# The causal mask of the attention maxima: by TensorE products with an identity, or inside VectorE's maximum instruction

## The chip, the cores and the metric

One Trainium2 chip, one of its cores. The metric is the device time of one launch in microseconds; lower is better. Times before the change are the median of three runs.

## The reference, cut to what matters

A two-layer post-norm decoder over 16 sequences of 512 tokens with 256 features. Each layer has causal self-attention, cross attention to 64 context tokens and a feed-forward part (a mixture of experts in layer 0, a wide hidden layer with sines in layer 1). The change concerns the causal self-attention of both layers, 16 heads of 16 features each:

```python
q, k, v = (heads(q), heads(k), heads(v))               # (batch, 16 heads, 512 tokens, 16)
logits = jnp.einsum('bhqd,bhkd->bhqk', q, k) * scale   # layer 0 adds a position bias
causal = jnp.tril(jnp.ones((t, t), dtype=bool))
logits = jnp.where(causal[None, None], logits, -jnp.inf)
attn = jax.nn.softmax(logits, axis=-1)
out = jnp.einsum('bhqk,bhkd->bhqd', attn, v)
```

## The kernel before, in words

**Recording and planning.** The kernel does not emit instructions as it goes. Each stage of each sequence records operations with an engine, a cost in microseconds and what they read and write. `stage` gives each operation a rank from the place of its stage and from a pair of offsets per kind of stage (`at`, `to`). `run_plan` then places all operations of all stages in one list, engine by engine, taking the earliest possible start and among those the lowest rank, and holding to the number of buffers of each pool. It emits them in that order, and every engine works through its own queue in that order. So the work of several sequences and stages is interleaved: between two pieces of one attention TensorE does expert products, projections or feed-forward products of others. All pinned instructions are issued by one helper line, which is why the profile names L347 for nearly everything; groups are told apart by their tiles.

**Causal attention** (`causal_attention`). The 16 heads are four groups of four heads; a group's heads lie on 32 partitions each. The scores are computed twice. The first time they are laid out with queries on partitions (`pa<-k,q` in the profile), only to find each query's maximum: `max_unit` fills one PSUM tile `pa` of 2 × 512 columns, one half for each head of a pair, and VectorE takes the maxima into `m`. The second time they are laid out with keys on partitions (`pa<-q,k`), in `exp_unit`: the maxima are subtracted (layer 0 through products `pa<-mrow,minus`, layer 1 inside `q` and `k`), ScalarE takes the exponential into `e`, GpSimd sets the part above the diagonal to zero, and TensorE multiplies by the values (`po<-e,vp`).

**Units.** A query block is 128 queries; block i needs the keys of blocks 0 to i, `kw = (i + 1) * 128` columns. `wide_banks` packs blocks into units of 512 columns per head: kind 0 is block 3 alone (512), kind 1 is blocks 2 and 0 (384 + 128), kind 2 is block 1 of two groups (256 + 256). With 16 sequences, two layers, and two pairs of groups and ten units per pair of groups (five kinds and groups, two pairs of heads) there are 640 max units and 640 exp units, each of 2 × 512 columns.

**Masking before.** In a max unit the last 128 columns of each block are the diagonal, where keys later than the query must not count. After the score products `masks()` adds a matrix of 0 and −1e30 there, by bf16 products with an identity that accumulate onto the scores in PSUM: one product per head and diagonal (kind 1's 384 block ends next to the 128 block's only columns, so that one product of 256 columns covers both diagonals). Then one `tensor_reduce` per block takes the maxima of both heads.

**Steps.** One step of the attention is one TensorE operation of one max unit and one exp unit (`score`), or of two of one kind when the other kind is not at hand. Its products run in three parts: the score products of all its units, then the maxima's subtraction, then the masks. Two `pa` tiles exist, so the next step's score products wait until VectorE has reduced the max unit and ScalarE has read the exp unit. When a group's maxima are complete, GpSimd copies them into a wide tile (`parts` in layer 0, `whole` in layer 1), TensorE transposes that (`pr`), and the group's exp units can begin.

Of the kernel before, what the change touches and what calls it, by code (L numbers as in the profile page):

```python
# [33 lines left out]
P = 128  # L34
# [36 lines left out]
def decoder_kernel(ctx: ExitStack, tc: tile.TileContext, a: dict, out: bass.AP):  # L71
# [15 lines left out]
    def whole_rows(key, name, shape):  # L87
# [17 lines left out]
    ident = const.tile([P, P], F32, tag="ident", name="ident")  # L105
    make_identity(nc, ident)

    cmask16 = const.tile([P, 2, P], BF16, tag="cmask16", name="cmask16")
    nc.gpsimd.memset(cmask16, 0.0)
    nc.gpsimd.affine_select(  # L110
        out=cmask16, in_=cmask16, compare_op=ALU.is_ge,
        fill=MASKED, base=0, pattern=[[0, 2], [-1, P]], channel_multiplier=1,
    )
    cmask16 = cmask16.rearrange("p n k -> p (n k)")

    vp = const.tile([P, NT, H, 2 * HD], F32, tag="vp", name="vp")
    nc.gpsimd.memset(vp, 1.0)
# [190 lines left out]
    def stage(place, record, *args):  # L308


        stage_ops.clear()
        record(*args)

        for t in loads.get(record.__name__, ()):
            for n in writers.get(t, ()) if isinstance(t, str) else ():
                for o in stage_ops:
                    if o.engine != "SP":
                        o.before.add(n)
                        ops[n].after.append(o.index)
                        o.left += 1  # L320
        loads.pop(record.__name__, None)

        tail, inside = {}, {o.index for o in stage_ops}
        for o in reversed(stage_ops):
            tail[o.index] = o.cost + o.wait + max((tail[n] for n in o.after if n in inside), default=0.0)
        longest = max(tail.values())
        done, total = 0.0, sum(o.cost for o in stage_ops if o.engine == "PE") or 1.0

        at, to = {a0: (-9.5, 0.0), a1: (-3.25, 0.55), c0: (-2.55, 0.65), ex: (-1.15, 1.8), c1: (-2.4, -0.65), ff: (-0.9, 8.5)}.get(
            record, (0.0, 1.0)  # L330
        )
        for o in stage_ops:
            o.rank = place + at + (to - at) * (done / total + 1.0 - tail[o.index] / longest) / 2
            if o.engine == "PE":
                done += o.cost
# [165 lines left out]
    def layernorm(x, t0, n, step=1):  # L501

        blocks = [t0 + step * t for t in range(n)]
        st = small([P, n, 6], f"st{n}", bufs=6, any_order=True)
        mv = small([P, n, 2], f"mv{n}", bufs=6, any_order=True)
        rs = small([P, n], f"rs{n}", bufs=6, any_order=True)
        for t in range(n):

            def stats(t=t):
                dve.bn_stats(st.t[:, t], x.t[:, blocks[t]])  # L510
                dve.bn_aggr(mv.t[:, t], st.t[:, t])

            op("DVE", 0.53, stats, [x[blocks[t]]], [st[t], mv[t]])
        op("DVE", 0.07, lambda: dve.tensor_scalar(rs.t, mv.t[:, :, 1], EPS, None, ALU.add),
           [mv[t] for t in range(n)], [rs])
        op("POOL", 0.35 + 0.15 * n, lambda: pool.tensor_tensor(rs.t, rs.t, minus_half[:, :n], ALU.pow), [rs], [rs])
        for t in range(n):
            DVE(
                D,
                lambda t=t: dve.tensor_scalar(  # L520
                    x.t[:, blocks[t]], x.t[:, blocks[t]], mv.t[:, t, 0:1], rs.t[:, t : t + 1],
                    ALU.subtract, ALU.mult,
                ),
                [rs, mv[t], x[blocks[t]]], [x[blocks[t]]],
            )
# [19 lines left out]

    def softmax(e, n, name):

        mx, sm = small([P, n], f"mx_{name}"), small([P, n], f"sm_{name}")
        cols = n * SK

        def wide(v):
            return v.unsqueeze(2).to_broadcast([P, n, SK])

        DVE(cols, lambda: dve.tensor_reduce(mx.t, e.t, AX.X, ALU.max), [e], [mx])
        POOL(cols, lambda: pool.tensor_tensor(e.t, e.t, wide(mx.t), ALU.subtract), [e, mx], [e], two=True)
        ACT(cols, lambda: act.activation(e.t, e.t, AF.Exp), [e], [e])
        DVE(cols, lambda: dve.tensor_reduce(sm.t, e.t, AX.X, ALU.add), [e], [sm])
        op("DVE", 0.02 + 0.0085 * n, lambda: dve.reciprocal(sm.t, sm.t), [sm], [sm])
        parts = 2 if cols > 512 else 1
        for m in range(parts):  # L560
            at = slice(m * n // parts, (m + 1) * n // parts)
            POOL(
                cols // parts, lambda at=at: pool.tensor_tensor(e.t[:, at], e.t[:, at], wide(sm.t)[:, at], ALU.mult),
                [e, sm], [e["half", m]], two=True,
            )
# [6 lines left out]
    def blocks_of(g, w):  # L572

        if w == 2:
            return [(g, 1, 0), (g + 1, 1, 256)]
        return [(g, i, at) for i, at in wide_banks[w]]

    def causal_attention(queries_keys, exact):
# [6 lines left out]
        def max_unit(g, w, pair):  # L585

            two = ps_a([P, 2, 512], "pa")
            lo = pair[0]

            diagonals = {0: [(384, 512)], 1: [(256, 512)], 2: [(128, 256), (384, 512)]}[w]  # L590
            own = sorted({b for b, _, _ in blocks_of(g, w)})


            def first():
                for b, i, at in blocks_of(g, w):
                    kw = (i + 1) * P
                    q, k = groups[b]["q"], groups[b]["k"]
                    for n, j in enumerate(pair):
                        rows = slice(32 * j, 32 * j + 32)
                        pe.matmul(  # L600
                            two.t[:, n, at : at + kw], q.t[rows, i * P : (i + 1) * P], k.t[rows, :kw],
                            start=at == 0, stop=False,
                        )

            def masks():
                for at, to in diagonals:
                    for n in range(2):
                        pe.matmul(
                            two.t[:, n, at:to], ident16, cmask16[:, : to - at],
                            start=False, stop=(at, to) == diagonals[-1],  # L610
                        )

            def follow():
                def reduce():
                    for b, i, at in blocks_of(g, w):
                        kw = (i + 1) * P
                        dve.tensor_reduce(
                            groups[b]["m"].t[:, i, lo : lo + 2], two.t[:, :, at : at + kw], AX.X, ALU.max
                        )

                DVE(
                    2 * sum((i + 1) * P for _, i, _ in blocks_of(g, w)), reduce, [two],
                    [groups[b]["m"][w, lo] for b in own], extra=0.075 * (len(blocks_of(g, w)) - 1),
                )

            return first, None, masks, follow, [t for b in own for t in groups[b]["ready"]], [two]

        def exp_unit(g, w, pair):

# [113 lines left out]
        def divided(g):  # L743
            os = groups[g]["os"]
            p = ps_d([P, 512], "pq")
            r = small([P, NT, NG, 1], "r")

            def turn():
                for i in range(NT):
                    pe.transpose(p.t[:, i * P : (i + 1) * P], os.t[:, i * P : (i + 1) * P], ident)  # L750

            PE(0.44, turn, [os], [p])

            def divide():
                p4 = p.t.rearrange("p (i j d) -> p i j d", j=NG, d=2 * HD)
                dve.reciprocal(r.t, p4[:, :, :, HD : HD + 1])
                dve.tensor_tensor(
                    y.t[:, :, g * 64 : (g + 1) * 64].rearrange("p i (j d) -> p i j d", d=HD),
                    p4[:, :, :, :HD],
                    r.t.to_broadcast([P, NT, NG, HD]),  # L760
                    ALU.mult,
                )

            op("DVE", 0.62, divide, [p], [r, *rows_of(y)] if g == 0 else [r, y[0, g]])
            if g:
                late.append(y[0, g])
# [15 lines left out]
        while last is None or n <= last:  # L782
# [9 lines left out]
                groups[g] = dict(q=q, k=k, ready=ready, m=small([P, NT, NG, 1], "m"))  # L792
            for g in [g for g, r in rows_at.items() if r == n]:
                rows_of_maxima(g)
            units, pace, masks, done = [], 0.0, 0.0, []
            for g, w, h in m_units[n_m : n_m + count_m]:
                units.append(max_unit(g, w, pairs[h]))
                pace, masks = 0.95, masks + (0.12 if w == 0 else 0.24)
                for b in sorted({b for b, _, _ in blocks_of(g, w)}):
                    finished[b] += 1  # L800
                    if finished[b] == 6:
                        done.append(b)
                        rows_at[b] = n + 2
# [6 lines left out]
            if units:  # L810
# [4 lines left out]
                            if u[part]:  # L815
                                u[part]()

                PE(pace + masks, score, [t for u in units for t in u[4]], [t for u in units for t in u[5]], kind="rows")
                for u in units:
                    u[3]()  # L820
            for g in done:
# [925 lines left out]
```

## Time and profile before

| what | value |
|---|---|
| median of three runs | 3836.05 us (3835.89 to 3839.94) |
| profiled execution, its own time | 3839.03 us |
| its span | 3837.3 us |
| granted TensorE clock, mean | 0.987 |
| TensorE products, busy | 3707.7 us (97%) |
| weight loads, busy | 2118.3 us (55%) |
| VectorE, busy | 2625.2 us (68%) |
| ScalarE, busy | 1474.9 us (38%) |
| GpSimd, busy | 1220.1 us (32%) |
| HBM traffic | 50 GB/s over the span |

Busy time is the union of the recorded spans of an engine's instructions. TensorE's products are pipelined, so their spans overlap and one product's span is longer than its share of the engine. A group's row reads: line, engine, operation, tile written <- tiles read, shape, count, then the group's busy time in us and the mean span of one in ns, then the idle time of the engine before it and who ended it. In the timeline a row reads: start, length in us, engine, line, operation, tiles, shape, number of instructions merged into the row. PE is TensorE's products, PEld its weight loads, DVE VectorE, ACT ScalarE, POOL GpSimd, SP the queue that issues most DMAs.

### The profile page before, as it was taken

How to read it: one execution, taken by the hardware profiler on the slowest of the kernel's cores; microseconds unless marked ns; L12 is line 12 of the kernel's file. 1: busy time of each engine (PE TensorE's matmuls, PEld its weight loads, DVE VectorE, ACT ScalarE, POOL GpSimd, SP SyncE). 2: the span in 40 equal slices, each digit the busy share in tenths (PEclk: the TensorE clock that was granted, in tenths of full speed). 3: DMA queues.
4: the chain of work that ended last, by engine and by line, in shares of the span. 5: the costliest groups of instructions: out<-in, count | busy, mean ns of one | idle time of the engine just before them, and what ended most of it. 6: DMA issues, size and time to landing. Idle time of an engine off the chain costs nothing.

```text
span 3837.3 us, 65114 instructions
## 1 busy us (share of the span) xinstructions
PE 3707.7 (97%) x26232; PEld 2118.3 (55%) x26232; DVE 2625.2 (68%) x5260; ACT 1474.9 (38%) x1988; POOL 1220.1 (32%) x2240
## 2 busy tenths in 40 slices
PE   8999999999999999999999999999999999999997
PEld 4555555555555555555555555555555555556554
DVE  3566667667686676867767686676866768677674
ACT  2333334335343343433435343353433434333353
POOL 2333122334232243323334233342322433233232
PEclk8999999999999999999999999999999999999998
DMA  4111211111111111111110111111111111111010
GB/s 166 35 46 31 67 58 59 53 59 31 45 55 57 63 46 41 42 56 58 50 59 25 50 59 54 58 36 40 55 57 63 45 44 44 50 59 43 26 39 11
DMA packets 101980, 195.12 MB, mean 51 GB/s; under 512 B 12112, under 2 KB 29536, under 8 KB 101680
## 3 DMA queue, kind: packets, MB, share of 16 engines
q1 hardware_dynamic: 99360, 183.02, 15.4%
q0 software_dynamic: 2000, 7.33, 0.6%
q8 instruction: 208, 3.41, 0.4%
q14 instruction: 92, 0.75, 0.1%
q10 hardware_dynamic: 320, 0.61, 0.0%
HBM read 148.45 MB, written 44.04 MB: 50 GB/s over the span
## 4 chain that ended last, share of the span: by engine, by line
PE 74%; DVE 13%; POOL 4%; ACT 4%; DMA 3%; issue 2%; SPq 0%; POOLq 0%; DVEq 0%; ACTq 0%
PE pa L347 20%; PE pf L347 8%; PE pg L347 7%; PE pu L347 7%; PE po L347 7%; PE pe L347 6%; PE pp L347 4%; PE pt L347 3%; PE pq L347 2%; DVE x L347 2%; DVE m L347 2%; ACT e L347 2%; PE pqk L347 2%; PE pv L347 2%; DVE act L347 2%
## 5 line engine op out<-in xcount | busy, mean ns | idle before, releaser
L347 ACT ACTIVATE e<-pa 128x1024 f32<-128x1024 f32 x640 | 636.7, 1021 | 701.1 <-PE pa L347 629.6
L347 DVE TENSOR_REDUCE m<-pa 128x2 f32<-128x1024 f32 (+3 forms) x1024 | 789.9, 815 | 168.8 <-PE pa L347 164.2
L347 POOL TENSOR_SCALAR_AFFINE_SELECT e<-e 128x256 f32<-128x256 f32 x1024 | 414.6, 425 | 918.4 <-ACT e L347 911.8
L347 PE MATMUL pa<-k,q 32*128 32x512 f32 (+3 forms) x4096 | 567.4, 469 | 20.1 <-DMA k<-way 9.2
L347 PE MATMUL pa<-q,k 32*128 32x512 f32 (+3 forms) x4096 | 554.7, 464 | 0.6 <-ACT e L347 0.3
L347 PEld LDWEIGHTS pa<-k,q 32*128 32x128 f32 x4096 | 273.8, 187 | 301.1 <-issue 198.8
L347 PE MATMUL po<-e,vp 128*32 128x512 f32 (+3 forms) x4096 | 355.5, 442 | 4.0 <-POOL e L347 2.9
L347 PE MATMUL pe<-xw,h 128*128 128x256 f32 x1280 | 332.3, 390 | 1.9 <-DVE x L347 1.0
L347 PE MATMUL pg<-xT,xw 128*128 128x512 f32 x640 | 309.1, 606 | 0.0
L347 PE MATMUL pu<-xT,xw 128*128 128x512 f32 x640 | 306.8, 602 | 0.7 <-DVE h L347 0.7
L347 PEld LDWEIGHTS pa<-q,k 32*128 32x128 f32 x4096 | 266.3, 185 | 71.6 <-issue 26.3
L347 ACT ACTIVATE h<-pg 128x512 f32<-128x512 f32 x160 | 95.5, 597 | 526.6 <-PE pg L347 526.6
L347 POOL TENSOR_TENSOR rs<-rs,minus_half 128x2 f32<-128x2 f32 x192 | 143.8, 753 | 439.4 <-DVE rs L347 436.1
L347 PEld LDWEIGHTS pe<-xw,h 128*128 128x128 f32 x1280 | 226.6, 190 | 91.0 <-issue 46.5
L347 PE MATMUL pf<-ff,act 128*128 128x256 f32 x1024 | 240.9, 389 | 9.8 <-DVE e L347 5.5
L347 DVE SCALAR_TENSOR_TENSOR x<-pe,r_pick,x 128x256 f32<-128x256 f32 x512 | 219.2, 476 | 35.3 <-PE pe L347 34.7
L347 PE MATMUL pf<-xT,L_ffn_W 128*128 128x512 f32 x512 | 242.2, 603 | 0.6 <-ACT act L347 0.5
L347 PEld LDWEIGHTS pf<-ff,act 128*128 128x128 f32 x1024 | 192.4, 193 | 46.7 <-DVE e L347 8.8
L347 DVE TENSOR_SCALAR x<-x,mv,rs 128x256 f32<-128x256 f32 x384 | 184.6, 515 | 46.1 <-POOL rs L347 44.9
L347 POOL TENSOR_TENSOR x<-x,rows 128x256 f32<-128x256 f32 x256 | 186.2, 756 | 91.7 <-PE pt L347 90.6
L347 PEld LDWEIGHTS <-ident 128*128 128x128 bf16 x1536 | 93.0, 98 | 201.2 <-issue 184.4
L347 PE MATMUL pa<-cmask,ident 128*128 128x128 bf16 (+1 forms) x1536 | 199.1, 242 | 0.0
(208 smaller groups left out, 5462.3 us busy)
## 6 DMA issues: line engine op xcount, KB each, us to landing
xw<-in_experts SPq DMA_DIRECT2D x160, 384.0 KB, 3.1
way<-qk SPq DMA_DIRECT2D x128, 256.0 KB, 3.3
q<-way SPq DMA_DIRECT2D x128, 256.0 KB, 3.1
k<-way SPq DMA_DIRECT2D x128, 256.0 KB, 4.2
x<-in_x SPq DMA_DIRECT2D x16, 512.0 KB, 4.1
out_x<-x SPq DMA_DIRECT2D x16, 512.0 KB, 2.9
ctx<-in_ctx SPq DMA_DIRECT2D x16, 64.0 KB, 2.2
x<-in_x POOLq DMA_DIRECT2D x1, 1024.0 KB, 6.9
```

What stands on the lines that cost most here:

```text
L347: return tc.keep_in_program_order(f(*args, **kw))
```

## The change

The mask products are gone, and VectorE adds the mask itself: instead of one reduction for two heads, one instruction for each head and block adds a mask to the scores (writing them back to PSUM) and accumulates the maximum. The mask is one bf16 tile of 512 columns, zero except in its last 128, and a block of `kw` columns reads its last `kw`. Each such call appears in the program as two VectorE instructions: one over the block, and one that writes the accumulated maximum to its column of `m`. The planner's costs follow, the stage offsets have other values, and some small buffers are fewer.

```diff
-    cmask16 = const.tile([P, 2, P], BF16, tag="cmask16", name="cmask16")
-    nc.gpsimd.memset(cmask16, 0.0)
+    cmask = const.tile([P, S], BF16, tag="cmask", name="cmask")
+    nc.gpsimd.memset(cmask, 0.0)
     nc.gpsimd.affine_select(
-        out=cmask16, in_=cmask16, compare_op=ALU.is_ge,
-        fill=MASKED, base=0, pattern=[[0, 2], [-1, P]], channel_multiplier=1,
+        out=cmask[:, S - P :], in_=cmask[:, S - P :], compare_op=ALU.is_ge,
+        fill=MASKED, base=0, pattern=[[-1, P]], channel_multiplier=1,
     )
...
-        at, to = {a0: (-9.5, 0.0), a1: (-3.25, 0.55), c0: (-2.55, 0.65), ex: (-1.15, 1.8), c1: (-2.4, -0.65), ff: (-0.9, 8.5)}.get(
+        at, to = {a0: (-7.8, -0.35), a1: (-3.75, 0.35), c0: (-2.15, 0.15), ex: (-1.2, 2.05), c1: (-3.0, 0.1), ff: (-1.85, 8.9)}.get(
...
-        st = small([P, n, 6], f"st{n}", bufs=6, any_order=True)
+        st = small([P, n, 6], f"st{n}", bufs=5, any_order=True)
...
-        mx, sm = small([P, n], f"mx_{name}"), small([P, n], f"sm_{name}")
+        mx, sm = small([P, n], f"mx_{name}", bufs=3), small([P, n], f"sm_{name}", bufs=3)
...
                         pe.matmul(
                             two.t[:, n, at : at + kw], q.t[rows, i * P : (i + 1) * P], k.t[rows, :kw],
-                            start=at == 0, stop=False,
-                        )
-
-            def masks():
-                for at, to in diagonals:
-                    for n in range(2):
-                        pe.matmul(
-                            two.t[:, n, at:to], ident16, cmask16[:, : to - at],
-                            start=False, stop=(at, to) == diagonals[-1],
+                            start=True, stop=True,
                         )
...
-                        dve.tensor_reduce(
-                            groups[b]["m"].t[:, i, lo : lo + 2], two.t[:, :, at : at + kw], AX.X, ALU.max
-                        )
+                        for n, j in enumerate(pair):
+                            dve.tensor_tensor_reduce(
+                                out=two.t[:, n, at : at + kw], in0=two.t[:, n, at : at + kw], in1=cmask[:, S - kw :],
+                                scale=1.0, scalar=LOWEST, op0=ALU.add, op1=ALU.max,
+                                accum_out=groups[b]["m"].t[:, i, j],
+                            )
 
                 DVE(
                     2 * sum((i + 1) * P for _, i, _ in blocks_of(g, w)), reduce, [two],
-                    [groups[b]["m"][w, lo] for b in own], extra=0.075 * (len(blocks_of(g, w)) - 1),
+                    [groups[b]["m"][w, lo] for b in own], extra=0.22 * len(blocks_of(g, w)) + 0.0,
                 )
...
-            r = small([P, NT, NG, 1], "r")
+            r = small([P, NT, NG, 1], "r", bufs=2)
...
-                pace, masks = 0.95, masks + (0.12 if w == 0 else 0.24)
+                pace = 0.95
...
-                PE(pace + masks, score, [t for u in units for t in u[4]], [t for u in units for t in u[5]], kind="rows")
+                PE(pace, score, [t for u in units for t in u[4]], [t for u in units for t in u[5]], kind="rows")
```

## The prediction

> **What bounds the kernel now.** I read the page first, then the groups of instructions with shapes kept apart, then the timeline of a few microseconds in the middle.
>
> ```profile
> span 3837.3 us, 65114 instructions
> PE 3707.7 (97%) x26232; PEld 2118.3 (55%) x26232; DVE 2625.2 (68%) x5260; ACT 1474.9 (38%) x1988; POOL 1220.1 (32%) x2240
> PE   8999999999999999999999999999999999999997
> DVE  3566667667686676867767686676866768677674
> PE 74%; DVE 13%; POOL 4%; ACT 4%; DMA 3%; issue 2%; SPq 0%; POOLq 0%; DVEq 0%; ACTq 0%
> ```
>
> TensorE is busy 97% of the span, in every slice, and is most of the chain that ended last. Its idle time is 3837.3 − 3707.7 = 130 us. By windows of 192 us, 22 us of that lie in the first, 33 us in the last and about 74 us in the eighteen between. So TensorE work taken out should shorten the span nearly one for one, as long as nothing else starts to hold TensorE up. VectorE is next at 68%, and 13% of the chain already runs over it, so the cover above it is not endless.
>
> ```profile
> L347 DVE TENSOR_REDUCE m<-pa 128x2 f32<-128x1024 f32 x256 | 306.0, 1216 | 73.7 <-PE pa L347 73.1
> L347 DVE TENSOR_REDUCE m<-pa 128x2 f32<-128x512 f32 x256 | 161.5, 683 | 34.8 <-PE pa L347 33.9
> L347 PE MATMUL pa<-cmask,ident 128*128 128x128 bf16 x1024 | 108.1, 223 | 0.0
> L347 PE MATMUL pa<-cmask,ident 128*128 128x256 bf16 x512 | 91.0, 281 | 0.0
> L347 DVE BATCH_NORM_AGGREGATE mv<-st 128x2 f32<-128x6 f32 x384 | 69.9, 182 | 13.1
> ```
>
> The first two rows give the maxima's price: (1216 − 683)/512 = 1.04 ns per element, and 683 − 533 = 150 ns fixed. The next two are what the change deletes: 1536 products. The last is the nearest row to a tiny VectorE instruction.
>
> ```profile
> 1007.04 0.40 PE L347 MATMUL pa<-cmask,ident 128*128 128x128 bf16 x4
> 1007.27 1.95 PE L347 MATMUL pp<-latproj,yT 128*128 128x256 f32 x8
> 1007.47 1.29 DVE L347 TENSOR_REDUCE m<-pa 128x2 f32<-128x512 f32 x2 [0.95 <-PE pa L347]
> 1009.15 0.70 PE L347 MATMUL pa<-k,q 32*128 32x512 f32 x2
> ...
> 1010.44 0.28 PE L347 MATMUL pa<-cmask,ident 128*128 128x128 bf16 x2
> 1010.44 0.18 DVE L347 BATCH_NORM_AGGREGATE mv<-st 128x2 f32<-128x6 f32 x1
> 1010.54 0.40 DVE L347 BATCH_NORM_STATS2 st<-x 128x6 f32<-128x256 f32 x1
> 1010.65 0.64 PE L347 MATMUL po<-e,vp 128*32 128x256 f32 x8
> ```
>
> Three things are to be seen. TensorE goes from mask products straight to other stages' products: four cost 1007.27 − 1007.04 = 0.23 us, two cost 0.21. The reduction ends at 1008.76 and the next products that need a score buffer start at 1009.15, so VectorE has 0.4 us to spare there. And VectorE overlaps neighbours: two reductions of 683 ns take 1.29, not 1.37, so one follows the other after 0.61; the 0.18 us aggregate lets the next start after 0.10.
>
> **Removed from TensorE.** Over all runs of mask products in the timeline I took the time from the first one's start to the next product's start. The median is 228 ns for the 256 runs of two, 327 ns for the 192 runs of four and 457 ns for the 32 runs of eight: 58.4 + 62.8 + 14.6 = **136 us**. The two rows above say 199 us of busy time, but their spans overlap the neighbours' ends; that is the upper end. Bare start-to-start times (56 and 119 ns) give 118 us, the lower end. The 1536 identity weight loads go with them; they lie beside products and I count nothing more for them. I take 137.
>
> **Added on VectorE.** The program has 1024 reductions fewer, and for each of 2048 heads-and-blocks one add-and-maximum plus one instruction that writes the accumulated maximum out to a single column: 4096 instead of 1024. The elements are the same, 640 units of 1024: 640 × 1024 × 1.04 ns = 682 us. The fixed part f of each such pair is on no row. Lower end: each follows its predecessor as tightly as the trace ever shows, 65 to 75 ns for a wide one (0.61 us less 0.53 of elements; I take 65) and 57 ns for the smallest (the 128x2 scalar operation of the layer norm): f = 0.122. Upper end: both pay everything alone, 150 + 150: f = 0.30. I take 65 + 100 (the aggregate) = 0.165, because that row is the nearest: tiny, and behind a producer. The sum is 682 + 2048 × 0.165 = 1020 us against 790 us busy for all reductions now (the page merges the forms), **+230 us** of VectorE (+142 and +506 at the ends). VectorE then stands at 2855 us, 77% of the new span.
>
> Here a rule speaks against the change. The Trainium skill (VectorE: DVE Perf Modes, "The DRAIN you can't avoid") says that the next operation waits until the pipe is empty, and its rules for authors say to minimize the count of operations; the same page says that an accumulator output is an instruction of its own, as the program here has it. By that rule f would be about 0.30 and the sum 1296 us. The 1.29 us row above shows the next one starting some 75 ns before the first ends, so I stay with 0.165 and keep 0.30 as the end. A second rule (Vector Engine (DVE) Microarchitecture Reference, "Points that are easy to get wrong") says that an instruction of two tensors and a scalar runs at half rate with two SBUF sources that are not bf16. Here one source is PSUM and the mask is bf16, so it should not bite; the nearest row, an operation on `h` and `pg` in fp32 with 512 elements, takes 683 ns, as long as the reduction. By the rule, the elements would cost 1364 us. No row shows this instruction writing to PSUM; that I take as part of f.
>
> **What hides it.** A unit now holds its score buffer for 1.07 us + 2f (one block) or + 4f (two blocks): 1.40 or 1.73 us, against 1.22 to 1.36. Behind it on VectorE's queue wait whatever evictions the plan put next (the `x`, `h`, `act` rows); TensorE waits for those and for the buffer. The order of the changed program differs all through, since the planner has new costs and stage offsets, so I counted it: for each of some 470 score steps with maxima, the TensorE work until the next score step, by start-to-start times of this trace. Steps with two units have a median of 2.60 us behind them before and 3.48 after; steps with one unit 2.67 and 2.62. Setting the units' time (plus 0.1 us to be seen; for two units less 0.5, as their first buffer is free sooner) against it, the shortfall sums to 18 us before, and after to 39 us at f = 0.122, 48 us at 0.165, 154 us at 0.30. So TensorE waits some **30 us more** (21 and 136 at the ends). A second way: 2% of the chain, 77 us, is `m`; 30% longer units make 23 us.
>
> **The small edits.** Layer norm's three small buffers go from six to five, the cross attention's two from four to three, `r` from four to two. The planner counts buffers, and the stretch from layer norm's statistics to its last use is short, so I cost them at nothing; uncovered, 192 layer norms at some 50 ns would be 10 us. The wider mask constant costs one GpSimd clear at the start. DMA issues are the same 612 SyncE instructions, only in another order, and DMA is 3% of the chain: nothing. New stage offsets change which stages overlap, ±20 us, and this goes into the range.
>
> **Sum.** 3839.0 − 137 + 30 = 3732 us on the profiled execution's own time, which stands 3.0 us above the median of the runs (3836.05): **3729 us**, I write 3730.
>
> **The rivals.**
> *VectorE's fixed price eats the gain.* With f = 0.30: 3839 − 137 + 136 = 3838, so 3835 as a median, no change. For it: 4096 instructions where 1024 were, 13% of the chain on VectorE. Against it: neighbours overlap in every VectorE group I saw. About 0.30 is also the point from which the change loses.
> *Half rate: slower.* If the add-and-maximum takes two cycles an element, a unit takes 2.13 us + 2f or 4f, VectorE works 2625 − 790 + 1364 + 338 = 3537 us, and the shortfall by the same count is 388 us, 370 more than now: 3839 − 137 + 370 = 4072, median 4069. The place is the score buffer; the sign turns when a two-block unit passes about 2.3 us. For it only the rule above, against it the fp32 two-source rows at one rate.
> *More gained.* f at its low end and all 199 us of the rows: 3839 − 199 + 21 = 3661. Unlikely, as the timeline shows overlap.
> *The change does not do what it says.* The program's counts show 1536 products gone and 4096 instructions come, so no chance is kept for that.
>
> **How the numbers follow.** The forecast (3690 to 3790) has 0.66, the eaten gain (3790 to 3880) 0.19, of which 0.06 is still faster, 0.03 no change and 0.10 slower; half rate (4000 to 4130) has 0.12, more gained 0.03. The range, 3690 to 3880, leaves out the last two, 0.15, and the tails. About 0.2% (8 us) is what a measurement can tell from no change. Faster: 0.66 + 0.06 + 0.03 = 0.75; within: 0.03; slower: 0.10 + 0.12 = 0.22.
>
> **What would show it.** Right: no `cmask,ident` products; TensorE busy near 3570 us and still 95% or more; a new group for the add-and-maximum of about 680 ns at 512 elements and one of 128x1 with short spans; VectorE near 2850 us; waits of TensorE for `m` up by tens of microseconds, not hundreds. Wrong: 1.1 us at 512 elements (half rate), or VectorE above 3100 us with TensorE below 93% and `m` large in the chain.

## The result, and the profile after

The changed kernel takes 3869.43 us (median of 4 runs, 3865.47 to 3871.51) against 3835.97 us before: ratio 1.0075, 95% interval 1.0063 to 1.0087 (the two medians alone divide to 1.0087). It is slower by 0.75%; 3730 us and faster was forecast. The profiled execution took 3867.62 us, its span is 3865.9 us.

The page of the changed kernel, the lines that answer to those of before:

```profile
span 3865.9 us, 64862 instructions
PE 3689.6 (95%) x24696; PEld 2075.3 (54%) x24696; DVE 2876.4 (74%) x8332; ACT 1477.2 (38%) x1988; POOL 1218.9 (32%) x2240
PE   8899999999999999999999999999999999999987
DVE  4676867778777687877778777686877778778774
PE 56%; DVE 32%; DMA 5%; issue 3%; ACT 3%; POOL 1%; SPq 0%; DVEq 0%; POOLq 0%; ACTq 0%
```

TensorE's products are 1536 fewer, and it is still shown busy 95% of a longer span. That figure deceives: a product that is held up between its neighbours adds to the union of recorded spans. The 4096 products `pa<-k,q` of the maxima are the same before and after, and their busy time went from 567.4 to 627.4 us. The chain that ended last says more: VectorE's share went from 13% to 32%, TensorE's from 74% to 56%. VectorE's own total rose by 251 us, about what was forecast (230).

The groups with shapes kept apart, in place of the old reductions:

```profile
L346 DVE CUSTOM_DVE_ANT_0 pa<-pa,cmask 128x512 f32<-128x512 f32 x512 | 353.3, 700 | 67.8 <-PE pa L346 59.0
L346 DVE DVE_READ_ACCUMULATOR2_ANT m<- 128x1 f32 x2048 | 289.2, 141 | 0.0
L346 DVE CUSTOM_DVE_ANT_0 pa<-pa,cmask 128x128 f32<-128x128 f32 x512 | 153.2, 299 | 17.4
```

The add-and-maximum takes 700 ns at 512 elements: (700 − 299)/384 = 1.04 ns an element, the rate that the reductions had. What is wrong stands between the instructions, in VectorE's timeline of one two-block unit:

```profile
1005.16 0.57 DVE L346 CUSTOM_DVE_ANT_0 pa<-pa,cmask 128x384 f32<-128x384 f32 x1 [0.80 <-PE pa L346]
1005.64 0.14 DVE L346 DVE_READ_ACCUMULATOR2_ANT m<- 128x1 f32 x1
1005.82 0.57 DVE L346 CUSTOM_DVE_ANT_0 pa<-pa,cmask 128x384 f32<-128x384 f32 x1
1006.30 0.14 DVE L346 DVE_READ_ACCUMULATOR2_ANT m<- 128x1 f32 x1
1006.48 0.30 DVE L346 CUSTOM_DVE_ANT_0 pa<-pa,cmask 128x128 f32<-128x128 f32 x1
1006.69 0.14 DVE L346 DVE_READ_ACCUMULATOR2_ANT m<- 128x1 f32 x1
1006.87 0.30 DVE L346 CUSTOM_DVE_ANT_0 pa<-pa,cmask 128x128 f32<-128x128 f32 x1
1007.08 0.14 DVE L346 DVE_READ_ACCUMULATOR2_ANT m<- 128x1 f32 x1
1007.08 0.60 DVE L346 CUSTOM_DVE_ANT_0 pa<-pa,cmask 128x384 f32<-128x384 f32 x1
```

Look at the starts. CUSTOM_DVE_ANT_0 is the add-and-maximum, DVE_READ_ACCUMULATOR2_ANT the write-out of its maximum. Inside the unit the next add-and-maximum starts 0.18 us after the start of the write-out (1005.64 to 1005.82, 1006.30 to 1006.48, 1006.69 to 1006.87). At the unit's end the next one starts with the write-out, at 1007.08. The instructions are the same, but the ones inside a unit wait for VectorE's own semaphore, a counter that the program lets VectorE raise and on which later instructions can be made to wait. In the changed program 1530 of the 2048 carry such a wait: all 1408 that follow another one of their unit, and 122 that begin a unit. Each of the 1408 writes the masked scores back into the `pa` tile that the one before it wrote too, and the program orders it behind that one though it goes to other columns. Over all units the medians from start to start are 784, 658, 525 and 392 ns for 512, 384, 256 and 128 columns inside a unit, which is 0.25 to 0.26 us beyond the elements, and 617, 350 and 217 ns at its end (512, 256 and 128 columns), 0.08 us beyond. In all four sizes the waiting instruction starts 34 ns (median) after the recorded end of the write-out.

Who let the score products' engine go, from the instructions that touch `pa` (idle time of an engine before them in us, and how often). First before, then the changed kernel's order with the old reductions and no mask (`a1_order_after_reductions_no_mask`, below), then the changed kernel:

```profile
  DVE m L347: 26.5, 40
```

```profile
  DVE m L346: 43.2, 44
```

```profile
  DVE m L346: 352.3, 457
```

Most of the last is on weight loads (75.7 us are on products), and a weight load's idle time alone doesn't show that the products behind it came later; the comparison of starts under the table of experiments 1 to 4 does. The chain in order of time, changed kernel, has ten microseconds that run over VectorE alone:

```profile
1004.04 1.09 PE pa L346 x16
1005.16 0.57 DVE pa L346
1005.82 0.57 DVE pa L346
1006.48 0.30 DVE pa L346
...
1009.18 1.14 DVE h L346 x2
...
1014.70 0.43 DVE pa L346
1015.25 1.13 PE pa L346 x4
```

Two units, then two evictions of `h` (finished products taken out of PSUM) and the router's small operations, then two more units; when the last frees its tile, the score products of 1015.25 can start. It is close to a tie, though. TensorE had work nearly all the while:

```profile
1008.71 1.66 PE L346 MATMUL pa<-k,q 32*128 32x256 f32 x16
1010.30 3.70 PE L346 MATMUL pu<-xT,xw 128*128 128x512 f32 x8
1013.93 1.13 PE L346 MATMUL pa<-k,q 32*128 32x512 f32 x4
1015.25 1.13 PE L346 MATMUL pa<-k,q 32*128 32x512 f32 x4 [0.19 <-DVE m L346]
```

Its recorded idle time before 1015.25 is 0.19 us. So a share of the chain says where time was tight, not how much was lost.

### The profile page after: what moved, and what is told of

It reads as the page before. It is cut to its first block, busy times and chain, and to the rows that moved or that the text cites. A ratio compares the mean times of both kernels' runs of the same rounds, so it can differ in the third digit from the quotient of the medians.

```text
span 3865.9 us, 64862 instructions
## 1 busy us (share of the span) xinstructions
PE 3689.6 (95%) x24696; PEld 2075.3 (54%) x24696; DVE 2876.4 (74%) x8332; ACT 1477.2 (38%) x1988; POOL 1218.9 (32%) x2240
## 4 chain that ended last, share of the span: by engine, by line
PE 56%; DVE 32%; DMA 5%; issue 3%; ACT 3%; POOL 1%; SPq 0%; DVEq 0%; POOLq 0%; ACTq 0%
DVE pa L346 14%; PE pa L346 14%; PE po L346 7%; PE pf L346 6%; PE pg L346 5%; PE pu L346 4%; PE pt L346 4%; PE pp L346 4%; PE pe L346 4%; DVE x L346 3%; DMA k<-way 3%; DVE m L346 2%; PE pq L346 2%; DMA way<-qk 2%; PE pqk L346 2%
## 5 line engine op out<-in xcount | busy, mean ns | idle before, releaser
L346 DVE CUSTOM_DVE_ANT_0 pa<-pa,cmask 128x512 f32<-128x512 f32 (+3 forms) x2048 | 1010.7, 500 | 151.8 <-PE pa L346 101.8
L346 PE MATMUL pa<-k,q 32*128 32x128 f32 (+3 forms) x4096 | 627.4, 478 | 94.3 <-DVE m L346 73.8
L346 POOL TENSOR_SCALAR_AFFINE_SELECT e<-e 128x256 f32<-128x256 f32 x1024 | 406.8, 417 | 733.9 <-ACT e L346 728.8
L346 PEld LDWEIGHTS pa<-k,q 32*128 32x128 f32 x4096 | 300.6, 191 | 414.0 <-DVE m L346 251.5
L346 DVE DVE_READ_ACCUMULATOR2_ANT m<- 128x1 f32 x2048 | 289.2, 141 | 0.0
L346 POOL CAST parts<-m 128x16 bf16<-128x16 f32 x192 | 49.0, 255 | 508.2 <-DVE m L346 361.6
L346 ACT ACTIVATE act<-pf,columns 128x512 f32<-128x512 f32 x128 | 87.8, 688 | 296.3 <-PE pf L346 296.1
```

What stands on the lines that cost most here:

```text
L346: return tc.keep_in_program_order(f(*args, **kw))
```

## Experiments 1 to 4: the same two orders, three ways to treat the mask

The order of instructions changed together with the instructions. These four runs take the two apart. Engine by engine the order of all other work is exactly that of the kernel before in the first two, and that of the changed kernel in the other two.

`b0_order_before_no_mask`: the kernel before, the body of the mask products gone, the planner's costs kept.

```diff
-                        pe.matmul(
-                            two.t[:, n, at:to], ident16, cmask16[:, : to - at],
-                            start=False, stop=(at, to) == diagonals[-1],
-                        )
+                        pass
```

> Order of the kernel before; the mask products are left out and nothing replaces them, so the maxima run over a whole diagonal block (the mask of the maxima is left out). This measures what the 1536 products are worth. If they cost what I read from their starts, 137 us, or the 109 us by which TensorE's start-to-start work fell in the changed kernel, the time is 3700 to 3730 us. If they lay largely in the shadow of other waits, 3780 us or more.

`b1_order_before_with_vector_mask`: the same, and the changed kernel's instruction, mask and small buffers. Those buffers by themselves leave the order as it was.

```diff
-                        dve.tensor_reduce(
-                            groups[b]["m"].t[:, i, lo : lo + 2], two.t[:, :, at : at + kw], AX.X, ALU.max
-                        )
+                        for n, j in enumerate(pair):
+                            dve.tensor_tensor_reduce(
+                                out=two.t[:, n, at : at + kw], in0=two.t[:, n, at : at + kw], in1=cmask[:, S - kw :],
...
```

> Order of the kernel before, engine by engine, with the add-and-maximum in place of products and reductions. Theory A (the two-block unit on VectorE, 1.93 us against 1.3, holds the score buffer and TensorE waits): slower than the changed kernel, since this order leaves only 2.6 us behind the steps with two units; 3890 to 3960 us. Theory B (the new stage offsets and order are what costs, not the instruction): 3730 to 3800 us.

`a1_order_after_reductions_no_mask`: the changed kernel, that same edit the other way round.

> Order of the changed kernel, with the old reductions and no mask in the maxima (the mask of the maxima is left out). Theory A: the waits for VectorE go and the gain of the missing products stays: 3690 to 3740 us. Theory B: the order itself is poor, so still 3800 us or more.

`a3_order_after_with_products`: the changed kernel, with `masks()` and the reductions of before.

> Order of the changed kernel with the old mask products and reductions. Theory A: the order as such is worth little either way, 3820 to 3860 us. Theory B: the order costs what the change lost, 3950 us or more (the 137 us that the prediction missed).

Measured, medians in us. The kernel before took 3841.58 beside these four.

| mask of the maxima | order before | order after |
|---|---|---|
| products and reductions | 3841.58 | 3806.87, ratio 0.9917 (0.9898 to 0.9935) |
| none, reductions | 3766.51, 0.9807 (0.9789 to 0.9824) | 3726.18, 0.9700 (0.9683 to 0.9717) |
| in VectorE's instruction | 4017.31, 1.0461 (1.0444 to 1.0478) | 3869.43 (its own comparison, above) |

Down the columns: the products are worth 75 us in the one order and 81 in the other, outside both expectations for the first run (3700 to 3730, or 3780 and more). The new instruction costs 251 us over the old reductions in the one order and 143 in the other (148 by the spans of the two profiled executions, since the medians come from two comparisons). Across the first row: the changed kernel's order is better by 35 us with everything else alike. So theory B, the order, fell on all three runs that put it. Theory A holds in kind, and in size for one run of three: it underrated the instruction in the old order (4017 against 3890 to 3960) and what the new order is worth (3807 against 3820 to 3860).

The chains of the two other runs in the order after, with products and then with no mask, to hold against the 32% above:

```profile
PE 86%; DMA 6%; DVE 3%; ACT 3%; issue 1%; POOL 0%; SPq 0%; POOLq 0%; DVEq 0%; ACTq 0%
```

```profile
PE 75%; DVE 12%; DMA 6%; ACT 3%; issue 2%; POOL 2%; SPq 0%; POOLq 0%; DVEq 0%; ACTq 0%
```

To see where the products' gain went, I split TensorE's time in each trace: for each kind of neighbouring products the lower quartile of start-to-start times over these six runs counts as its own time, the rest as waiting. Some of that rest is pace and not waiting: score products start in fours some 7 ns apart, and for 256 columns the next four come 209 ns later. So only the differences between runs are to be read.

| profiled run | own time, us | waiting, us |
|---|---|---|
| before | 3157 | 667 |
| order before, no mask | 3033 | 722 |
| order after, products | 3144 | 655 |
| order after, no mask | 3020 | 683 |
| order after, VectorE's mask | 3008 | 844 |
| order before, VectorE's mask | 3025 | 980 |

Without products, TensorE's own time falls by 124 us in both orders, but waiting grows by 55 and 28. That it comes sooner to buffers which other engines have not freed is likely, and was not shown by itself. VectorE's instruction adds 161 us of waiting in the order after.

Where those stand can be read without any split. "Order after, no mask" and "order after, VectorE's mask" run the same products in the same order, and from first to last start the second takes 149 us more. Of these, 93 us lie before `pa<-k,q` and 36 before `pa<-q,k`, the products that fill the two `pa` tiles; all others together have 20. So the score buffer that VectorE holds is the place. The granted clock fell from 0.983 to 0.978 between the two; on a span of 3718 us that makes some 19 us by estimate, spread over all products, and cannot be the rest.

## Experiments 5 and 6: taking away the wait inside a unit

Nobody reads the masked scores. They can be written to spare tiles in turn, and then successive instructions have no tile in common that both write. The spare tiles need 4 KB per partition, which one `e` buffer fewer gives; `e0_five_e_buffers` is the changed kernel with that alone, and the next run has its exact order.

```diff
-    e_pool, os_pool = Pool("e", 6), Pool("os", 1)
+    e_pool, os_pool = Pool("e", 5), Pool("os", 1)
```

> The changed kernel with five e buffers instead of six, the control for the next run, which needs that space. The planner's order changes with it. Expected 3860 to 3900 us.

`e1_sums_to_spare_tiles`, in which a counter advances with each call and picks the tile:

```diff
+    spill = [const.tile([P, S], BF16, tag=f"spill{n}", name=f"spill{n}") for n in range(4)]
...
-                                out=two.t[:, n, at : at + kw], in0=two.t[:, n, at : at + kw], in1=cmask[:, S - kw :],
+                                out=spill[turn_of_spill[0] % 4][:, :kw], in0=two.t[:, n, at : at + kw], in1=cmask[:, S - kw :],
```

> As the control, in the same order, but the masked scores that nobody reads are written to four spare bf16 tiles in turn instead of back over the scores, so that an add-and-maximum does not wait for the one before it in the same score tile. Theory A1 (the wait within a unit, about 170 ns for 1408 of 2048 blocks, is most of what the instruction costs beyond the reductions): a two-block unit falls from 1.93 us to about 1.4, and the time 60 to 110 us below the control. Theory A2 (the pair of instructions is long in itself, a wait or not): blocks still follow each other after 0.26 us and more beyond their elements, and the time is within 20 us of the control.

The control took 3897.88 us (ratio to before 1.0158, 1.0137 to 1.0179). With spare tiles it is **3741.72 us**, ratio 0.9751 (0.9725 to 0.9778): 156 us less from one operand, more than A1 expected. VectorE's timeline of the run with spare tiles, a two-block unit:

```profile
1009.12 0.56 DVE L349 CUSTOM_DVE_ANT_0 spill<-pa,cmask 128x384 bf16<-128x384 f32 x1
1009.60 0.08 DVE L349 DVE_READ_ACCUMULATOR2_ANT m<- 128x1 f32 x1
1009.60 0.55 DVE L349 CUSTOM_DVE_ANT_0 spill<-pa,cmask 128x384 bf16<-128x384 f32 x1
1010.08 0.08 DVE L349 DVE_READ_ACCUMULATOR2_ANT m<- 128x1 f32 x1
1010.08 0.29 DVE L349 CUSTOM_DVE_ANT_0 spill<-pa,cmask 128x128 bf16<-128x128 f32 x1
1010.29 0.08 DVE L349 DVE_READ_ACCUMULATOR2_ANT m<- 128x1 f32 x1
1010.29 0.29 DVE L349 CUSTOM_DVE_ANT_0 spill<-pa,cmask 128x128 bf16<-128x128 f32 x1
```

Each write-out starts together with the next add-and-maximum: it costs no time of its own. The medians from start to start are 611, 478, 344 and 211 ns, 0.078 us beyond the elements everywhere. From its first start to the start of its last write-out the unit takes 1.38 us (1009.12 to 1010.50), where the changed kernel took 1.92 (1005.16 to 1007.08). The union of all maxima on VectorE is 880 us, against 1121 in the control, and from first to last start TensorE's products take 159 us less than in the control, 91 of them before `pa<-k,q` and 34 before `pa<-q,k`.

A wait on the semaphore as such is not what costs. In this run 763 of the 1408 calls inside a unit still carry one, for an earlier instruction that is over by then, and they follow their predecessors as fast as those without (478 and 477 ns at 384 columns, 211 and 211 at 128).

## Experiments 7 and 8: the wait or the PSUM write

Two things changed at once in the last run: no wait for the call just before, and no write to PSUM. One spare tile brings the wait back without the PSUM write; two are the least that can alternate.

```diff
-    spill = [const.tile([P, S], BF16, tag=f"spill{n}", name=f"spill{n}") for n in range(4)]
+    spill = [const.tile([P, S], BF16, tag=f"spill{n}", name=f"spill{n}") for n in range(1)]
...
-                                out=spill[turn_of_spill[0] % 4][:, :kw], in0=two.t[:, n, at : at + kw], in1=cmask[:, S - kw :],
+                                out=spill[turn_of_spill[0] % 1][:, :kw], in0=two.t[:, n, at : at + kw], in1=cmask[:, S - kw :],
```

The other run has 2 in both places.

> As the run with four spare tiles, in the same order, but with one spare tile: the masked scores leave PSUM alone, yet each add-and-maximum again waits for the one before it, which wrote the same tile. If the wait is the cause (theory A1), blocks follow each other 0.19 to 0.26 us beyond their elements and the time goes back towards the control's 3898 us, 3840 to 3920 us. If writing back to PSUM was the cause, the time stays at 3735 to 3760 us.

> The same with two spare tiles in turn. The wait is then for the instruction before the previous one, which is over by the time: as with four, 3730 to 3755 us, with half of their space. If two are too few, between that and the run with one.

One tile: 3870.0 us, ratio 1.0073 (1.0056 to 1.009). Two tiles: 3746.46 us, 0.9753 (0.9737 to 0.977). VectorE's timeline with one tile:

```profile
1005.34 0.68 DVE L349 CUSTOM_DVE_ANT_0 spill<-pa,cmask 128x512 bf16<-128x512 f32 x1
1005.94 0.08 DVE L349 DVE_READ_ACCUMULATOR2_ANT m<- 128x1 f32 x1
1006.06 0.69 DVE L349 CUSTOM_DVE_ANT_0 spill<-pa,cmask 128x512 bf16<-128x512 f32 x1
```

The next start is again 0.12 us behind the start of the write-out, and with it the run takes 124 us more than with two tiles. The three runs with spare tiles differ in nothing but their number, so the wait is the cause. Where the scores are written plays a smaller part, through the same wait: the waiting instruction starts 34 to 35 ns after the write-out's end in both cases, and the write-out lasts 141 ns in the control and 82 ns here. Blocks of 512 follow each other after 784 ns (fp32 to PSUM) and 734 ns (bf16 to a spare tile), and one tile is 28 us better than the control. Place and type changed together; no run parts them.

## Experiments 9 and 10: the plan

`a2_planner_told_the_cost` tells the planner what the units take; `o1_before_with_new_offsets` asks what made the changed order the better one.

```diff
-                    [groups[b]["m"][w, lo] for b in own], extra=0.22 * len(blocks_of(g, w)) + 0.0,
+                    [groups[b]["m"][w, lo] for b in own], extra=0.27 if w == 0 else 0.80,
```

> The changed kernel, with the planner told what its units take on VectorE (1.40 and 1.93 us instead of 1.35 and 1.57). Theory C (the loss is the plan's: it expected VectorE 0.36 us sooner in 384 units): 3790 to 3830 us. Theory A (a unit that holds its score buffer so long costs TensorE however it is planned): 3840 to 3890 us.

> The kernel before with the changed kernel's stage offsets alone. If the offsets made the order that was worth 35 us, 3795 to 3815 us; if the higher cost of VectorE's maxima in the plan made it, 3825 to 3850 us.

The first took 3970.31 us (ratio 1.0338, 1.0322 to 1.0354): worse than either theory allowed, with true costs. The second, the kernel before with the changed `at` and `to`, took 3862.97 us (1.0058, 1.004 to 1.0077): the offsets alone make the old plan worse, so neither of its two readings fits. It may be that offsets and costs fit each other only as a set; one `e` buffer fewer moved the changed kernel by 28 us as well. Why the true cost gives so bad an order was not tried further and stays open. What the first settles is only that the loss was not repaired by telling the planner of it; what made the 35 us is open too.

## Why the prediction was wrong

**The bound: right, but read too generously.** TensorE is the engine to relieve: without products and with nothing in their place the kernel gains in both orders. But neither 97% busy nor 74% of the chain told how much of a cut arrives.

**Removed from TensorE: mis-sized.** The prediction took 137 us for the products, one for one. Own time fell by 124, and 75 to 81 us of it arrived in the medians. In the profiled executions, which the split above describes, 68 and 96 us arrived and 55 and 28 came back as waits. The step that failed here was the sentence that work taken out shortens the span nearly one for one.

**Added on VectorE: wrong in kind.** The prediction sought one fixed part f per block, between 0.122 and 0.30 us, and took 0.165 from neighbours that do not wait for each other. There are two values: 0.08 where nothing is waited for, below its lower end, and 0.26 inside a unit. The average over 1408 blocks inside and 640 at the end is 0.20. The waits were there to be read in the changed program before the run; the diff shows why, since `out` is the tile that all of a unit's calls write. The prediction wrote that what writing to PSUM costs is part of f and never asked what the next instruction would wait for. It also said that neighbours overlap in every VectorE group it saw. They do not, and the row before its own excerpt of the kernel before shows it:

```profile
1009.98 0.43 DVE L347 BATCH_NORM_STATS2 st<-x 128x6 f32<-128x256 f32 x1
1010.44 0.18 DVE L347 BATCH_NORM_AGGREGATE mv<-st 128x2 f32<-128x6 f32 x1
1010.54 0.40 DVE L347 BATCH_NORM_STATS2 st<-x 128x6 f32<-128x256 f32 x1
```

The aggregate reads what the statistics wrote, waits for them on VectorE's semaphore, and starts after their end at 1010.41; all 384 aggregates of that trace start 34 ns after it. The next statistics do not wait for the aggregate and start 0.08 us before it ends. The price of a wait, nearly 0.12 us, was in the trace of before.

**What hides it: the largest miss, and the step that turned the sign.** 30 us of waiting were forecast; the instruction cost 143 us over reductions in the same order. Only a part of that is f: the prediction's own count gives 30 us at 0.165 and 136 at 0.30, and it bends upward, so at 0.20 it would have given 58 at most. The rest is the count itself. It set a unit's time against the TensorE work behind the step and gave the evictions on VectorE's queue no time, although it named them; in the chain from 1005 to 1015 us two evictions and a router stand between the units. How much of the miss that is was not measured. VectorE's total was nearly right (2876 us against 2855) by luck: the maxima alone went from 790 us to 1121, 331 more where 230 were forecast, and the rest of VectorE's busy time came out lower by 80.

**The two rules.** By the prediction's reading of the Trainium skill's drain rule (VectorE: DVE Perf Modes, "The DRAIN you can't avoid") f was to be 0.30. That reading left out a sentence of the same paragraph, that a next operation that is not held back starts earlier, and this is what the trace shows without a wait: f is 0.078 to 0.084. Inside a unit, with the wait, 0.26 comes near 0.30 for another reason. The same section measured eight copies, with a semaphore after each and with one after the last alone, and found that it costs nothing extra; here a wait for the instruction just before costs 0.12 to 0.17 us, and a wait for an older one nothing. The half-rate rule (Vector Engine (DVE) Microarchitecture Reference, "Points that are easy to get wrong") did not bite (1.04 ns an element), and its condition, two SBUF sources that are not bf16, was not met, so this case does not test it.

**Rivals and offsets.** The rival "VectorE's fixed price eats the gain" came closest (3790 to 3880, 0.19), with its mechanism, the score buffer held too long, though not its cause. The new order was allowed ±20 us and gave 35 us of gain. In runs: −35 for the order, −81 for the products and +143 for the instruction make +28 against the 3841.58 us measured beside them. The three steps lead from one end of the table to the other, so that sum is no test; the +33 of the result differs only because the kernel before took 3835.97 us beside it.

**A version that beats both.** VectorE's mask with spare tiles, 3741.72 us. What the instruction still costs there was not measured, since no run has the reductions with five `e` buffers. Leaving the mask out of the maxima altogether is faster still (3726.18 us): subtracting a larger number than the maximum leaves a softmax unchanged so long as no row's exponentials vanish. That depends on the data, and so it stays an experiment.

## What to carry to other kernels

When an instruction gets an output that nobody reads, look at what that output makes the next instruction wait for, and give it a tile of its own; here two in turn suffice. Before costing a chain of instructions on one engine, list the waits each carries on its own engine's semaphore: here the next instruction came 0.12 to 0.17 us later with a wait for the one just before. And price a buffer by when it comes free, not by the engine's total: here 259 us more of VectorE's busy time cost 143 us in one order, and 290 us more cost 251 in the other.

## What was not expected of the hardware

The write-out of the accumulator costs nothing when the next instruction does not wait: both start in the same 10 ns, and the pair advances at 611 ns for 512 elements, where the plain two-input operations `h<-h,pu` and `h<-h,pg` of the trace before, where nothing holds the next one up, need 595 and 605. An instruction that does not wait starts some 83 ns before the recorded end of the one before it; one that waits for it starts 34 ns after. VectorE's wait for its own last instruction costs 167 ns when that wrote to PSUM and 123 ns when it wrote bf16 to SBUF (784 − 617, 734 − 611), and the write-out itself lasts 141 ns after the one and 82 ns after the other. The granted TensorE clock was lower in the runs with more waiting, 0.987 before, 0.978 after, 0.977 with VectorE's mask in the order before and 0.973 with the planner told the cost; why is not shown.
